# K of the second group multiplied ahead of Q from the weight blocks still in SBUF, with Wo and W1 loaded later and the prologue reordered

## The chip, the cores and the metric

One core of a Trainium2 chip. The metric is the device time of one execution in microseconds; the time of a kernel is the median of its runs. TensorE (PE), VectorE (DVE), ScalarE (ACT) and GpSimd (POOL) each take their own instructions in order; SyncE's queue (SP) issues nearly all DMAs, in order too.

## The reference

x is 128 graphs of 128 nodes with 512 features (f32), adj a 128x128 mask for each graph. Two layers, each with its residual and layer norm:

```
q, k, v = x@Wq + bq, x@Wk + bk, x@Wv + bv              # 8 heads of 64
logits  = where(adj > 0, q@k.T / 8, -1e9)
x = layernorm(x + relu(softmax(logits) @ v @ Wo + bo))

Wh = x @ W1
e  = where(adj > 0, leaky(Wh@a1 [:, None] + Wh@a2 [None, :]), -9e15)
x = layernorm(x + leaky(softmax(e, axis=1) @ Wh))
```

## The kernel before

**Work and stages.** Graphs go in groups of four (512 rows). For group 0 the prologue multiplies Q, K and V in the plain way; for each later group they are made by a two-level Strassen-Winograd scheme. A weight matrix then becomes 49 blocks of 128x128: 7 outer places (`low`/`high`, lines 268 to 315) by 7 inner ones, the sums built once in place. Blocks of Wq stay in SBUF for the whole kernel. Blocks of Wk and Wv are built (`wk.build.0` to `.7` on DVE, `wv.build` on POOL), written to DRAM (`wk.store`, `wv.store`), and fetched back for every group, since the bytes they were built in are used again.

**Where the blocks lie.** Wk is loaded into and built in the tile `late` (`wo_w` in the profile); Wo and W1 go into the same bytes afterwards. Wo's seven places cover exactly `wk.low`, W1's cover `wk.high`. `w.load` issues the four loads of Wo, `w.w1_load.n` those of W1 (and two of its vectors a), `w.block.n` builds Wo's four further places on DVE. Wv is built in `arena`.

**The chains.** A group is six chains, numbered c: two for each matrix (r = 0 with four inner products for each outer one, r = 1 with three, the remainder). `chain_name` says which matrix. A chain has seven outer products in the order p1, p5, p6, p2, p7, p4, p3 (`STEPS`), into three PSUM banks named y, w and x (tags a, b, c, turned by c). Copies from the y bank (t0, t2, t3, c21) are ScalarE's; sums (c11, c22, c12) are DVE's; p6 follows on p1 in the bank y and needs t0 read, p7 needs t2, p4 needs t3. When a chain is done, 3 to 6 combinations finish its output. r = 0 of the first matrix keeps its second half in a spare tile, because the four graphs of the group before still read the output tile.

**Fetches.** `fetch_until` fetches the blocks of chains that are `streamed`: before, K and V of every group from the second on, one or two places at a time, 256 to 512 KB (r = 0) or 192 to 384 KB (r = 1), three ahead.

**Order of work.** Nothing is scheduled by a program at run time: `BEGIN`, a text of some 500 tokens, is the order in which the prologue's instructions are issued, and each engine takes its own in that order. The tokens that matter here:

- `y.q.n.half`, `y.k.n`, `y.v.b`: group 0's products on TensorE; `y.oq.n`, `y.ok.n`, `y.ov.b`: ScalarE's copies of them. n = 2o + j: product n reads of the places 2o and 2o+1 the inner columns j and j+2 (`turned_product`, line 1354). Banks are those of the chains for n < 3, another one for n = 3.
- `wk.build.0` (line 288): inner column 1 minus column 0 in the outer places 0 to 3, in place; `.1` to `.4` whole places (512 wide); `.5` to `.7` further inner columns (896 wide).
- `bN.load`, `bN.turn`: x of graph N fetched and turned on DVE; `bN.masks`, `bN.cast`, `bN.mask`: the adjacency fetched (two graphs at once), cast on ScalarE, made a mask on DVE.
- `sN.scores` (TensorE, 16 matmuls), `sN.add` and `sN.reduce` (DVE: mask and maximum), `sN.exp`, `sN.divide` (ScalarE, by heads), `sN.reciprocals` (DVE), `sN.store`/`sN.fetch`/`sN.transpose` (through DRAM), `sN.attend` (TensorE): attention of graph N.
- `g1.n`, `i1.sNa`, `i1.sNb`: sums of the second group's x that its chains read, on POOL, or on DVE with `.v`.
- `h`: the next product of the chains; `a`, `d`: the next of ScalarE's and DVE's pieces left by it; `k`, `k.v`: the next combination on POOL or DVE; `q`: the next fetch.
- `zN.p1` and so on: Wo's product for a pair of graphs (layer 0's end); `zN.by`, `zN.bw` set its biases in a bank.

After the prologue a steady loop with its own order runs to the end; its text is not touched.

The lines that say which blocks a product reads:

```
block = w.place(2 * o + c // 2).rearrange("p (c f) -> p c f", c=2)
... block[:, c % 2, j * P : (j + 1) * P]                       # group 0

return ring[c, f"p{n + 1}"][:, (0, 1, 2, 0, 3, 1, 2)[m], :]    # a chain, from fetched blocks
```

Of the kernel before, what the change touches and what calls it, by code (L numbers as in the profile page):

```python
# [20 lines left out]
BIG = -1e30  # L21

BEGIN = """
    y.q.1.0 y.q.0.0 y.order.2 b0.masks y.order.3 y.rows.2 y.rows.3 y.q.2.0 y.q.1.1 y.q.2.1
    y.k.3 y.k.1 b4.load.1 y.oq.1 b1.cast b0.cast y.oq.2 b5.load.2 y.k.2 b6.load.0 b2.masks
    w.bias y.q.3.0 y.q.0.1 y.q.3.1 b4.turn wk.build.0 b5.turn b6.turn b7.load.1 wk.build.1
    wk.build.2 wk.build.3 b3.cast wk.build.4 b0.mask b2.cast y.k.0 b1.mask b7.turn
    wk.build.5 y.ok.3 y.oq.0 y.ok.1 y.oq.3 y.ok.2 y.ok.0 wq.scale.3 wq.scale.2 g1.0
    b8.load.2 b4.masks wq.scale.0 wq.scale.1 g1.2 g1.1 b9.load.0 s0.scores wk.build.6
    wk.build.7 s0.add.1 s0.add.0 g1.3 i1.s1a i1.s1b s1.scores s0.reduce s1.add.1 s1.add.0  # L30
    s1.reduce b2.mask wq.build.0 s0.exp.6.7 s0.exp.0.1 s0.exp.2.3 s0.exp.4.5 wk.store.0
    wk.store.2 i1.s3a s0.reciprocals.1 wq.build.1 s0.reciprocals.0 i1.s3b.v wq.build.2 y.v.1
    y.v.3 y.v.0 y.v.2 wk.store.1 wk.store.3 wq.build.4 wq.build.3 w.load w.w1_load.2
    w.w1_load.0 q q b10.load.1 i1.s2a.v i1.s2b w.w1_load.7 q b6.masks w.w1_load.4 wq.build.5
    wq.build.6 b3.mask i1.s4a.v i1.s4b h s2.scores s0.divide.0.1 s1.exp.5.6 s1.exp.2 b4.cast
    s1.exp.7 s1.exp.3.4 s0.divide.4.5 s0.divide.6.7 b5.cast s1.exp.0.1 s0.divide.2.3
    s1.reciprocals.1 b5.mask w.block.0 wq.build.7 w.w1_load.5 s0.store w.w1_load.1
    w.w1_load.6 s1.divide.6.7 b8.turn s1.reciprocals.0 w.w1_load.3 h b11.load.2 y.ov.1
    y.ov.0 y.ov.2 b6.cast a s0.fetch b7.cast s1.divide.4.5 wv.build.0 wv.build.1 h
    wv.build.2 s1.divide.0.1 s1.divide.2.3 a b6.mask s2.add.1 b10.turn s2.add.0 s2.reduce h  # L40
    h h s2.exp.0.1 s2.exp.4.5 a a s2.exp.2.3 d w.halve d s0.transpose b4.mask b11.turn
    s2.reciprocals.0 b9.turn h s3.scores h h h h s0.attend wv.build.3 wv.build.4 wv.build.5
    q s1.store wv.store.2 wv.store.0 s2.exp.6.7 a wv.build.6 wv.build.7 s2.divide.2.3 z0.bw
    s2.divide.0.1 a z0.by wv.store.1 wv.store.3 h h a a s1.fetch h d s3.add.0 s3.add.1 d
    s2.reciprocals.1 k.v w.block.1 k.v d h h s3.reduce a h d b7.mask w.block.2 k.v w.block.3
    q k k k s0.copy s2.divide.6.7 s2.divide.4.5 a h h s1.transpose s3.exp.2 s3.exp.0.1
    y.ov.3 a s3.exp.5.6 z1.by s3.exp.3.4 w.w1_load.8 w.w1_load.9 d d w.w1_sum.3 w.w1_sum.2
    z0.p2 h h s1.attend h a s3.exp.7 a q s2.store g2.0 q q q s3.reciprocals.0 s2.fetch k k.v
    k k.v w.w1_sum.5 s3.reciprocals.1 b1.residual s3.divide.2 s1.copy s1.sum.0 s1.sum.1
    s1.sum.2 z0.p1 h h h s3.divide.3.4 z1.bw z0.t0 s3.divide.7 s3.divide.0.1 a s3.divide.5.6  # L50
    d z0.p5 h w.w1_sum.0 d w.w1_sum.6 k.v w.w1_sum.1 a z0.p6 d z0.c11 z0.t2 k s1.sum.3
    s2.transpose g2.1 k h z0.p7 h h d a z0.t3 a z0.p4 s2.attend z0.c22 k.v z0.c21 s2.copy k
    z0.p3 s3.store b0.residual q z0.stats.1 z0.rstd.1 s3.fetch z0.c12 z1.p1 z0.stats.0 k
    g2.2 q q q k g2.3 z0.apply.1 s3.transpose h h s4.scores s4.add.0 s4.add.1 s3.attend
    z0.rstd.0 z1.t0 a h h s3.copy s4.reduce s4.exp.4.5 s4.exp.0.1 w.w1_sum.4 s5.scores
    b12.load.2 q z0.store.1 b3.residual q h a s4.exp.2.3 s3.sum.0 s4.exp.6.7 s3.sum.1
    s3.sum.2 d z0.apply.0 d w.w1_sum.8 s5.add.1 s5.add.0 s4.reciprocals.1 h a a h s3.sum.3
    z1.p6 h z1.p5 h w.w1_sum.9 s4.reciprocals.0 s5.reduce i2.s1b d w.w1_sum.7 s4.divide.4.5
    s4.divide.6.7 k.v i2.s1a.v k.v s4.divide.0.1 s4.divide.2.3 z1.t2 z1.p7 s5.exp.3.4
    s5.exp.6.7 z1.t3 z0.store.0 q h i2.s3b s5.exp.2 a s4.store s5.exp.5 s5.exp.0.1 z1.p4 h  # L60
    i2.s2a z0.fetch_both a s4.fetch d w.w1_sum.11 i2.s3a.v s5.reciprocals.1 h z1.c21
    w.w1_block.0 s5.reciprocals.0 z1.c22 d h k.v s5.divide.2 s5.divide.7 s5.divide.3.4
    s5.divide.0.1 h s5.divide.5.6 i2.s2b z1.p3 z1.p2 a a i2.s4a s5.store h z1.stats.1 q
    b2.residual d z0.transpose.0 b12.turn h h s4.transpose z1.c11 w.w1_sum.10 k.v k.v k k
    s5.fetch a h z0.transpose.1 z1.rstd.1 w.w1_block.1 s4.attend d z0.sum.0 z0.sum.2 a
    b13.load.0 z1.c12 d i2.s4b w.w1_block.3 z0.sum.1 q q b14.load.2 h h h h s4.copy a a
    z1.stats.0 s5.transpose s5.attend s5.copy d z1.rstd.0 z1.apply.1 k.v k.v z0.sum.3
    s5.sum.0 b13.turn s5.sum.2 w.w1_block.2 z1.store.1 s5.sum.1 k s5.sum.3
"""

STEADY = {
# [94 lines left out]
def kernel(  # L166
# [84 lines left out]
    PLACE = (0, 1, 3, 6, 2, 5, 4)  # L251
# [67 lines left out]
    wq = Weights(const.tile([P, 49 * P], F32, name="wq"))  # L319
    OUTER = 7 * D  # L320
    late = const.tile([P, 2 * OUTER + 14], F32, name="wo_w1")
    wk = Weights(late)
# [3 lines left out]
    wv = Weights(arena)  # L326
# [80 lines left out]
    X, XT, XS, INNER, Q, K, V, MF, OT, X1T, X1, WH = ({} for _ in range(12))  # L407
# [175 lines left out]
        return [step(names) for names in ORDER]  # L583

    def chain_name(c):
        return "QKV"[c % 6 // 2]

    OUT = {"Q": Q, "K": K, "V": V}
    outputs = {
# [12 lines left out]
    def sequence():  # L602
# [10 lines left out]
    streamed = [  # L613
        (c, name)
        for c, name in all_steps
        if c >= 6 and c % 6 >= 2 and name in ("p1", "p5", "p2", "p4")
    ]
    place_in_stream = {step: j for j, step in enumerate(streamed)}

    def fetch_until(last):  # L620
        while fetched[0] <= min(last, len(streamed) - 1):
            c, name = streamed[fetched[0]]
            r = c % 2
            names = (name,) if name == "p1" else (name, CHAIN[CHAIN.index(name) + 1])
            at = [PLACE[PRODUCTS[n]] for n in names]
            low, high = min(at), max(at)
            blocks = work.tile([P, 2, 4, P], F32, name="w_n", bufs=AHEAD + 1)
            for n, place in zip(names, at):
                ring[c, n] = blocks[:, int(place > low)]
            src = stored["w" + chain_name(c).lower(), r][low : high + 1 : max(high - low, 1)]  # L630
            nc.sync.dma_start(blocks[:, : len(at), : 4 - r, :], src.rearrange("n p i f -> p n i f"))
            fetched[0] += 1

    def cells(c):

        g, name = c // 6, chain_name(c)
        if c % 2 == 0:
            if g not in OUT[name]:
                OUT[name][g] = outputs[name]

            def place(h, o):
                if h == 0 or name != "Q":
                    return OUT[name][g][:, h, :, o, :]
                if c not in spare_cells:
                    t = work.tile([P, 2, 3, 2, P], F32, name="cells")
                    flat = t.rearrange("p h s o t -> p (h s o t)")[:, : 8 * P]
                    spare_cells[c] = flat.rearrange("p (s o t) -> p s o t", s=4, o=2)
                return spare_cells[c][:, :, o, :]

            return place  # L650
        if c not in spare_cells:
            spare_cells[c] = work.tile([P, 2, 3, 2, P], F32, name="cells")
        return lambda h, o: spare_cells[c][:, h, :, o, :]

    def group_product(c):
        g, r, name = c // 6, c % 2, chain_name(c)
        count = 4 - r
        outer_tile = {}
# [5 lines left out]
        def weight(n, m):  # L664
            if name == "Q":
                return wq.inner(m)[:, PLACE[n], :]
            return ring[c, f"p{n + 1}"][:, (0, 1, 2, 0, 3, 1, 2)[m], :]

        def multiply(p, n, start):
            j = place_in_stream.get((c, f"p{n + 1}"))  # L670
            if j is not None and not steady[0]:
                fetch_until(j + AHEAD)
            operand = INNER[g][1]
            for index, m in enumerate(ROUNDS[r]):
                xs = operand(n, INNER_PLACE.index(m))
                w = weight(n, m)
                lhs, rhs = (xs, w) if name == "V" else (w, xs)
                nc.tensor.matmul(  # L678
                    p[:, index, :],
                    lhs,  # L680
                    rhs,
                    start=start and index == 0,
                    stop=True,
                    skip_group_check=True,
                )
# [1066 lines left out]
```

## Time and profile before

| | |
|---|---|
| median of three runs | 2266.84 us (2261.54 to 2272.79) |
| the profiled execution | 2263.41 us, span 2261.6 us |
| granted TensorE clock, mean | 0.998 |
| DMA | 540.78 MB, mean 239 GB/s |
| first 300 us: PE busy | 288.39 us |
| first 300 us: DMA | 73.40 MB, 245 GB/s |
| Wo's loads issued | 40.41 to 44.15 us |
| first fetch of K's blocks | 46.50 us |
| first product of the second group | 54.67 us |

A line of the waits view says who waited for whom: us in total, times, the longest. A line of the timeline has the start, the length, engine, line, operation, output<-inputs, shape, count, and in brackets the idle time before it with what ended it. Matmuls of f32 take two instructions for one logical product of 128 rows.

### The profile page before, as it was taken

What the parts mean: (1) busy time and instruction counts of PE and PEld (TensorE: products, weight loads), DVE (VectorE), ACT (ScalarE), POOL (GpSimd) and SP (SyncE); (2) the same over time, 40 slices, a digit from 0 to 9 for tenths busy, and PEclk for the clock granted to TensorE, in tenths of its full rate; (3) what the DMA queues carried; (4) which work ended last, traced back from release to release, by engine and by line L of the source; (5) the groups of instructions that cost most, each with busy time, mean ns of one, the idle gap of its engine ahead of it and who ended that gap; (6) DMA issues with size and microseconds to landing.
All of it is one profiled execution on the core that took longest, in us unless ns stands there. A gap on an engine that the chain in (4) does not pass through costs nothing.

```text
span 2261.6 us, 52550 instructions
## 1 busy us (share of the span) xinstructions
PE 2236.6 (99%) x17228; PEld 2015.0 (89%) x17228; DVE 2014.3 (89%) x4225; ACT 1661.6 (73%) x5955; POOL 1406.2 (62%) x1697
## 2 busy tenths in 40 slices
PE   9899999999999999999999999999999999999998
PEld 6889999999999999999899999999999999999985
DVE  5889999999988999988999889999899988899977
ACT  3668777677677787776776777877767767778786
POOL 2666666656766566666567665666665676556656
PEclk9999999999999999999999999999999999999999
DMA  9988788887888888888888888888888888888764
GB/s 230 273 238 239 237 245 248 240 249 231 243 244 250 247 239 239 241 247 242 235 237 245 241 249 246 239 239 246 244 241 247 235 243 239 250 247 237 219 214 151
DMA packets 516592, 540.78 MB, mean 239 GB/s; under 512 B 100568, under 2 KB 394336, under 8 KB 516320
## 3 DMA queue, kind: packets, MB, share of 16 engines
q1 hardware_dynamic: 516000, 537.17, 81.3%
q8 instruction: 137, 2.24, 0.4%
q14 instruction: 135, 1.11, 0.2%
q10 hardware_dynamic: 320, 0.26, 0.0%
HBM read 388.96 MB, written 148.31 MB: 238 GB/s over the span
## 4 chain that ended last, share of the span: by engine, by line
PE 89%; DMA 4%; DVE 4%; ACT 1%; SPq 1%; issue 1%; POOL 0%; POOLq 0%; DVEq 0%; ACTq 0%
PE st_y L678 24%; PE p_y L798 19%; PE st_w L678 12%; PE p_w L798 9%; PE st_x L678 6%; PE lg L872 6%; PE p_oT L952 5%; PE p_x L798 5%; PE p_h L1207 4%; DMA adj<-in_adj_dram 1%; DMA paz<-pa_dram 1%; DMA w_n<-wv 0%; SPq L933 0%; ACT pa L920 0%; DVE pa L939 0%
## 5 line engine op out<-in xcount | busy, mean ns | idle before, releaser
L906 ACT ACTIVATE pa<-pa,nmax 128x128 f32<-128x128 f32 x1000 | 391.8, 397 | 11.7 <-DVE nmax L895 9.4
L920 ACT ACTIVATE pa<-pa,rs 128x128 f32<-128x128 f32 x1000 | 327.2, 401 | 4.1 <-DVE rs L916 4.1
L728 POOL TENSOR_TENSOR out_Q<-out_Q,cells 128x512 f32<-128x512 f32 x92 | 116.2, 1277 | 297.4 <-DVE out_Q L728 297.4
L691 ACT COPY cells<-st_y 128x384 f32<-128x384 f32 x279 | 133.0, 477 | 102.6 <-PE st_y L678 101.9
L967 ACT ACTIVATE arena<-p_oT,b_cols 128x128 f32<-128x128 f32 x504 | 138.1, 382 | 80.6 <-PE p_oT L952 79.7
L906 ACT ACTIVATION_READ_ACCUMULATOR pa<-pa,nmax 128x1 f32 x1000 | 193.4, 193 | 0.0
L1008 POOL TENSOR_TENSOR rstd<-ve,mhalf 128x1 f32<-128x1 f32 x256 | 161.4, 631 | 21.3
L1000 DVE BATCH_NORM_STATS2 st<-arena 128x6 f32<-128x512 f32 x248 | 168.8, 681 | 1.2
L1006 POOL TENSOR_SCALAR ve<-mv 128x1 f32<-128x1 f32 x256 | 76.1, 297 | 147.7 <-DVE mv L1002 145.0
L886 DVE TENSOR_TENSOR pa<-lg,mf 128x512 f32<-128x512 f32 x250 | 161.5, 675 | 3.7 <-PE lg L872 3.7
L939 DVE STREAM_TRANSPOSE pa<-paz 128x1024 f32<-128x1024 f32 x125 | 154.6, 1236 | 7.0 <-DMA w_n<-wv 3.0
L895 DVE TENSOR_REDUCE nmax<-pa 128x8 f32<-128x1024 f32 x125 | 151.0, 1208 | 1.2
L872 PE MATMUL lg<-out_K,out_Q 64*128 64x128 f32 x2048 | 139.6, 281 | 0.7 <-ACT out_K L1391 0.7
L872 PEld LDWEIGHTS lg<-out_K,out_Q 64*128 64x128 f32 x2048 | 125.2, 187 | 14.3 <-issue 7.2
L728 POOL TENSOR_TENSOR out_K<-out_K 128x512 f32<-128x512 f32 x62 | 79.1, 1275 | 91.1 <-DVE out_K L728 91.1
L712 DVE TENSOR_TENSOR cells<-st_w,cells 128x384 f32<-128x384 f32 (+1 forms) x217 | 120.9, 557 | 16.6 <-ACT cells L691 16.3
L798 PE MATMUL p_y<-wo_w,x1T 128*128 128x257 f32 x496 | 134.2, 393 | 0.0
L1214 ACT ACTIVATE arena<-p_h 128x512 f32<-128x512 f32 x120 | 71.9, 599 | 83.8 <-DMA out_dram<-arena 60.2
L798 PE MATMUL p_y<-wo_w,arena 128*128 128x256 f32 x504 | 131.3, 383 | 0.9 <-ACT pr_t L809 0.9
L1021 DVE TENSOR_SCALAR arena<-arena,mv,rstd 128x512 f32<-128x512 f32 x239 | 131.2, 549 | 0.6 <-POOL rstd L1008 0.6
L798 PE MATMUL p_y<-wo_w,oS 128*128 128x256 f32 x504 | 129.8, 380 | 0.1
L798 PE MATMUL p_y<-wo_w,x1S 128*128 128x257 f32 x496 | 128.2, 380 | 0.2 <-ACT arena L809 0.2
(301 smaller groups left out, 7720.8 us busy)
## 6 DMA issues: line engine op xcount, KB each, us to landing
paz<-pa_dram SPq DMA_DIRECT2D x504, 128.0 KB, 3.6
pa_dram<-pa SPq DMA_DIRECT2D x125, 512.0 KB, 3.8
w_n<-wk SPq DMA_DIRECT2D x93, 512.0 KB, 4.3
w_n<-wv SPq DMA_DIRECT2D x93, 512.0 KB, 5.1
w_n<-wk SPq DMA_DIRECT2D x93, 384.0 KB, 4.3
w_n<-wv SPq DMA_DIRECT2D x93, 384.0 KB, 3.5
x_dram<-arena SPq DMA_DIRECT2D x128, 256.0 KB, 2.6
xz<-x_dram SPq DMA_DIRECT2D x240, 128.0 KB, 3.8
```

Source lines behind the costliest of these rows:

```text
L678: nc.tensor.matmul(p[:, index, :], lhs, rhs, start=start and index == 0, stop=True, skip_group_check=True,)
L728: (by or engine).tensor_add(*(t(n) for t, n in (dst, left, right)))
L798: nc.tensor.matmul(p[:, :width], xs()[n][:, kc, :], w[:, PLACE[n], kc, :], start=start and kc == 0, stop=True, skip_group_check=True,)
L872: nc.tensor.matmul(self.lg[r][:, c, :], q[rows, 2 * (b % 2) + c % 2, c // 2, :], k[rows, 2 * (b % 2) + c % 2, c // 2, :], start=c == 0, st ...
L886: nc.vector.tensor_add(by_head[:, r * NC : (r + 1) * NC], self.lg[r].rearrange("p c (b k) -> p c b k", b=4), mf.unsqueeze(1).to_broadcast( ...
L895: nc.vector.tensor_reduce(self.nmax, by_head, AX.XY, ALU.max, negate=True)
L906: nc.scalar.activation(self.pa[:, :, h, :], self.pa[:, :, h, :], AF.Exp, bias=self.nmax[:, h : h + 1], accum_out=self.sums[:, h : h + 1],)
L920: nc.scalar.activation(self.pa[:, :, h, :], self.pa[:, :, h, :], AF.Copy, scale=self.rs[:, h : h + 1])
L939: nc.vector.transpose(self.paT.rearrange("p h (a i) -> p a h i", i=32), self.paz.rearrange("p a (h k) -> p a h k", k=32),)
L967: nc.scalar.activation(OT[pair][:, c, h * P : (h + 1) * P], self.oT[:, c, :], AF.Identity, bias=b_cols[:, 1, c : c + 1],)
L1000: nc.vector.bn_stats(st, self.src)
L1008: nc.gpsimd.tensor_tensor(self.r, ve, mhalf, ALU.pow)
```

## The change

1. `chain_name`: the second group (c = 6 to 11) takes its matrices in the order K, Q, V, all other groups Q, K, V as before.
2. K's two chains of the second group (c = 6, 7) read the blocks of `wk` where they were built; `streamed` begins with c = 8 and leaves out Q, so eight fetches go.
3. The spare tile for the second half goes with the first chain of a group, whichever matrix it is.
4. `BEGIN` has a new order. Wo and W1 are loaded after K's chains of the second group, which read the bytes they go to. Eight `q` are gone, three `k.v` are `k`, and `i1.s1b`, `i1.s2b`, `i1.s4b` carry `.v`; all other tokens are the same ones in another order.

```diff
 BEGIN = """
-    y.q.1.0 y.q.0.0 y.order.2 b0.masks y.order.3 y.rows.2 y.rows.3 y.q.2.0 y.q.1.1 y.q.2.1
-    y.k.3 y.k.1 b4.load.1 y.oq.1 b1.cast b0.cast y.oq.2 b5.load.2 y.k.2 b6.load.0 b2.masks
-    w.bias y.q.3.0 y.q.0.1 y.q.3.1 b4.turn wk.build.0 b5.turn b6.turn b7.load.1 wk.build.1
-    wk.build.2 wk.build.3 b3.cast wk.build.4 b0.mask b2.cast y.k.0 b1.mask b7.turn
-    wk.build.5 y.ok.3 y.oq.0 y.ok.1 y.oq.3 y.ok.2 y.ok.0 wq.scale.3 wq.scale.2 g1.0
-    b8.load.2 b4.masks wq.scale.0 wq.scale.1 g1.2 g1.1 b9.load.0 s0.scores wk.build.6
-    wk.build.7 s0.add.1 s0.add.0 g1.3 i1.s1a i1.s1b s1.scores s0.reduce s1.add.1 s1.add.0
...
+    y.q.0.0 y.q.1.0 b0.masks y.order.2 y.rows.2 y.order.3 y.rows.3 y.q.2.0 y.q.2.1 y.q.0.1
+    y.q.1.1 y.k.3 y.q.3.0 y.k.1 b6.load.0 w.bias b5.load.2 b4.load.1 b2.masks y.k.2 y.q.3.1
+    y.oq.2 wq.scale.1 b0.cast y.oq.0 y.oq.1 b1.cast wq.scale.0 b2.cast b3.cast y.ok.2 y.oq.3
+    wq.scale.2 y.ok.3 y.ok.1 b6.turn b4.turn b9.load.0 b7.load.1 y.k.0 wk.build.0 b5.turn
+    wk.build.1 wk.build.2 wq.scale.3 y.ok.0 wk.build.3 wk.build.4 wk.build.5 wk.build.7
+    b3.mask b7.turn b0.mask s0.scores s1.scores s0.add.0 s0.add.1 y.v.1 y.v.0 wk.store.1
+    b8.load.2 s0.reduce b1.mask s1.add.0 s1.add.1 wq.build.0 wk.store.0 b4.masks b10.load.1
+    s0.exp.4.5 s0.exp.6.7 s0.exp.2.3 s0.exp.0.1 s0.reciprocals.1 s1.reduce s0.reciprocals.0
+    wq.build.1 g1.2 g1.0 g1.1 g1.3 i1.s1a s0.divide.4.5 s0.divide.6.7 s0.divide.2.3
+    s1.exp.5.6 s1.exp.2 y.v.2 y.v.3 s0.divide.0.1 i1.s2a.v i1.s1b.v wq.build.2 b4.cast
+    s1.exp.7 s1.exp.3.4 y.ov.0 i1.s3a wk.build.6 wq.build.3 b5.cast s1.exp.0.1 wq.build.4
+    i1.s4a.v wq.build.5 i1.s2b.v s2.scores h h wq.build.7 i1.s4b.v b2.mask s1.reciprocals.1
+    b8.turn s1.reciprocals.0 w.halve s2.add.0 s2.add.1 s0.store y.ov.1 s1.divide.4.5
+    s1.divide.6.7 s1.divide.2.3 s1.divide.0.1 y.ov.2 a h wk.store.3 s0.fetch b6.masks
+    wv.build.0 s2.reduce wv.build.1 wv.build.2 a z0.by s2.exp.2.3 s2.exp.6.7 s2.exp.4.5
+    wk.store.2 b11.load.2 h h s2.exp.0.1 b6.cast a s1.store s0.transpose i1.s3b.v
+    s2.reciprocals.1 d s2.reciprocals.0 b10.turn b9.turn b4.mask d wv.build.4 wv.build.3
+    s0.attend h h s3.scores h a s2.divide.2.3 y.ov.3 h h z1.bw a b7.cast s2.divide.0.1 a
+    s2.divide.6.7 z0.bw h h h wv.build.5 a s2.divide.4.5 a wv.build.7 wv.build.6 wv.store.2
+    wv.store.0 h wv.store.1 s1.fetch d k.v k.v d s3.add.1 s3.add.0 k.v d h b11.turn
+    s3.reduce d h h a wv.store.3 s1.transpose b5.mask wq.build.6 s0.copy s3.exp.0.1 a h h
+    s1.attend s3.exp.5.6 s3.exp.2 s3.exp.3.4 w.load k k k g2.0 a s3.exp.7 s1.copy k s1.sum.0
+    s2.store w.w1_load.2 w.w1_load.1 w.w1_load.3 w.w1_load.5 w.w1_load.8 w.w1_load.0
+    w.w1_load.9 d k.v w.block.0 k.v k.v s1.sum.2 s1.sum.1 z0.p1 h h z0.p2 s3.reciprocals.1
...
     def chain_name(c):
-        return "QKV"[c % 6 // 2]
+        return ("KQV" if c // 6 == 1 else "QKV")[c % 6 // 2]
...
-        if c >= 6 and c % 6 >= 2 and name in ("p1", "p5", "p2", "p4")
+        if c >= 8 and chain_name(c) != "Q" and name in ("p1", "p5", "p2", "p4")
...
-                if h == 0 or name != "Q":
+                if h == 0 or c % 6:
                     return OUT[name][g][:, h, :, o, :]
...
             if name == "Q":
                 return wq.inner(m)[:, PLACE[n], :]
+            if c < 8:
+                return wk.inner(m)[:, PLACE[n], :]
             return ring[c, f"p{n + 1}"][:, (0, 1, 2, 0, 3, 1, 2)[m], :]
```

More of the change, by code (lines that the diff above doesn't have):

```diff
@@ L30 @@
-    wk.build.7 s0.add.1 s0.add.0 g1.3 i1.s1a i1.s1b s1.scores s0.reduce s1.add.1 s1.add.0
[L31 to L65, printed above, removed]
@@ L66 @@
-    b13.load.0 z1.c12 d i2.s4b w.w1_block.3 z0.sum.1 q q b14.load.2 h h h h s4.copy a a
-    z1.stats.0 s5.transpose s5.attend s5.copy d z1.rstd.0 z1.apply.1 k.v k.v z0.sum.3
-    s5.sum.0 b13.turn s5.sum.2 w.w1_block.2 z1.store.1 s5.sum.1 k s5.sum.3
+    y.q.0.0 y.q.1.0 b0.masks y.order.2 y.rows.2 y.order.3 y.rows.3 y.q.2.0 y.q.2.1 y.q.0.1
+    y.q.1.1 y.k.3 y.q.3.0 y.k.1 b6.load.0 w.bias b5.load.2 b4.load.1 b2.masks y.k.2 y.q.3.1
+    y.oq.2 wq.scale.1 b0.cast y.oq.0 y.oq.1 b1.cast wq.scale.0 b2.cast b3.cast y.ok.2 y.oq.3
@@ new lines @@
+    s1.attend s3.exp.5.6 s3.exp.2 s3.exp.3.4 w.load k k k g2.0 a s3.exp.7 s1.copy k s1.sum.0
+    s2.store w.w1_load.2 w.w1_load.1 w.w1_load.3 w.w1_load.5 w.w1_load.8 w.w1_load.0
+    w.w1_load.9 d k.v w.block.0 k.v k.v s1.sum.2 s1.sum.1 z0.p1 h h z0.p2 s3.reciprocals.1
+    w.block.1 s3.reciprocals.0 d w.block.2 h s3.divide.2 z0.t0 a a s3.divide.7 s3.divide.5.6
+    s3.divide.3.4 s3.divide.0.1 h z0.p6 h a s2.fetch w.w1_load.4 w.w1_load.7 q w.w1_load.6
+    s3.store b1.residual h h z0.p5 w.block.3 z0.c11 d b6.mask k.v w.w1_sum.1 d z0.t2 a d
@@ new lines @@
+    s2.transpose w.w1_sum.6 w.w1_sum.2 w.w1_sum.3 s1.sum.3 z0.p7 h h z0.t3 z1.by a a z0.p4 h
+    s2.attend d z0.c22 w.w1_sum.0 k k g2.1 z0.c21 q b0.residual h k.v k z0.stats.1 z0.p3 h
+    z0.c12 s4.scores s3.fetch q w.w1_sum.5 s2.copy a z0.rstd.1 s4.add.0 s4.add.1
+    s3.transpose z1.p1 h h k g2.2 k s3.attend z0.apply.1 z0.stats.0 s5.scores s3.copy z1.t0
+    a s4.reduce q b12.load.2 q q z0.store.1 s4.exp.0.1 s4.exp.6.7 s4.exp.2.3 h z1.p2 h
+    z0.rstd.0 g2.3 s3.sum.0 s3.sum.2 s3.sum.1 d s5.add.1 z0.apply.0 s4.exp.4.5 a a d b7.mask
@@ new lines @@
+    z1.c11 h q b3.residual z0.store.0 z1.p6 s4.reciprocals.0 w.w1_sum.4 s4.reciprocals.1 d
+    s5.add.0 s5.reduce s4.divide.6.7 s4.divide.4.5 z1.t2 s4.divide.0.1 w.w1_sum.7 k s3.sum.3
+    s4.divide.2.3 z1.p5 h h q z0.fetch_both i2.s1a.v w.w1_sum.11 k.v i2.s2a k i2.s1b i2.s2b
+    z1.p7 h s5.exp.5 a z1.t3 s5.exp.3.4 s5.exp.6.7 h z1.c22 z1.p4 i2.s4a s5.exp.2 a
+    s5.exp.0.1 s5.reciprocals.1 d z1.c21 w.w1_sum.9 s5.reciprocals.0 d w.w1_sum.10
+    z1.stats.1 z0.transpose.1 h h h s5.divide.5.6 s5.divide.0.1 s5.divide.7 s5.divide.3.4
@@ L69 @@
+    s5.divide.2 s4.store b2.residual z1.p3 a s4.fetch h h d z0.transpose.0 w.w1_sum.8
+    s5.store a a z1.rstd.1 k.v k.v s4.transpose i2.s3a.v b12.turn h h s4.attend h b13.load.0
+    s5.fetch z1.apply.1 d k k a a z1.c12 d z1.stats.0 h h w.w1_block.0 i2.s4b i2.s3b
+    s5.transpose d z0.sum.2 z1.rstd.0 z0.sum.0 a s4.copy h z0.sum.1 w.w1_block.1 s5.attend
+    s5.copy k w.w1_block.2 w.w1_block.3 s5.sum.0 s5.sum.1 z0.sum.3 s5.sum.2 q q q b14.load.2
+    z1.store.1 s5.sum.3 k k b13.turn
 """
```

## The prediction

> **What bounds the kernel now.** I read the page first, then TensorE's waits in the first 300 us, then the windows round the longest of them, and last the timeline of 24 to 66 us, where the change acts.
>
> ```profile
> span 2261.6 us, 52550 instructions
> ...
> PE 2236.6 (99%) x17228; PEld 2015.0 (89%) x17228; DVE 2014.3 (89%) x4225; ACT 1661.6 (73%) x5955; POOL 1406.2 (62%) x1697
> ...
> PE   9899999999999999999999999999999999999998
> ```
>
> TensorE is the bound: it idles 25.0 us of 2261.6. Everything the change touches lies in the first two or three of the forty slices (56.5 us each). Its waits there:
>
> ```profile
> PE st_y L678 <- ACT out_Q L697: 2.1, 1, 2.1
> PE st_w L678 <- DVE cells L712: 1.5, 1, 1.5
> PE p_busy L1316 <- POOL ident masks.py:199: 1.3, 1, 1.3
> PE st_y L678 <- DVE cells L712: 1.3, 1, 1.3
> PE st_y L678 <- ACT out_V L1412: 1.0, 1, 1.0
> PE p_oT L952 <- DVE arena L939: 0.9, 1, 0.9
> PE st_y L678 <- DVE out_K L712: 0.9, 1, 0.9
> PE lg L872 <- ACT out_K L1391: 0.7, 1, 0.7
> ```
>
> With four shorter ones and a few cracks the timeline's gaps add up to 11.6 us by 145.8 us: 1.3 at the start, 3.9 more up to 60.15, 6.3 after. No DMA is a releaser: the fetches that the change removes stop TensorE only through other engines. One does: at 59.0 ScalarE has waited 3.9 us for a mask (adj) that lay behind the loads of Wk's blocks, Wo and W1, and the 2.1 us wait is behind that. It is followed by a half clock:
>
> ```profile
> 58.20:61.60 3.40, 1.45 (x12) 1.45 (x13) 2.26 (x4) 2.59 (x10) 3.24 (x4) 0.97 0.74 208
> 61.60:65.00 3.40, 3.33 (x16) 3.04 (x16) 3.33 (x4) 2.88 (x14) 3.32 (x2) 0.52 0.76 196
> ```
>
> (columns: length, busy time of PE, PEld, DVE, ACT, POOL, granted clock, DMA share, GB/s). 3.4 us at 0.5 cost 1.7. So all that can be won is 10.3 of gaps and 1.7 of clock, 12.0 us or 0.53%.
>
> **Part 1, the four K products and DVE's first build.** This is the step that I count on.
>
> ```profile
> 24.67 3.70 PE L1360 MATMUL st_x<-xT,wo_w 128*128 128x512 f32 x8
> 26.92 1.02 PE L1360 MATMUL st_x<-xT,wo_w 128*128 128x512 f32 x2
> 27.55 0.69 DVE L288 TENSOR_TENSOR wo_w<-wo_w 128x512 f32<-128x512 f32 x1 [2.34 <-PE st_x L1360]
> 32.83 5.20 DVE L288 TENSOR_TENSOR wo_w<-wo_w 128x896 f32<-128x896 f32 x3
> 33.38 3.60 PE L1360 MATMUL st_y<-xT,wo_w 128*128 128x512 f32 x8
> 38.87 1.29 DVE L886 TENSOR_TENSOR pa<-lg,mf 128x512 f32<-128x512 f32 x2 [0.83 <-PE lg L872]
> 41.44 0.40 ACT L906 ACTIVATE pa<-pa,nmax 128x128 f32<-128x128 f32 x1 [1.75 <-DVE nmax L895]
> 60.15 0.49 PE L678 MATMUL st_y<-xS,wq 128*128 128x128 f32 x2 [2.13 <-ACT out_Q L697]
> ```
>
> wk.build.0 (27.55) changes in place only column 1 of places 0 to 3. k.2 reads columns 0 and 2 of places 2 and 3, none of them; yet DVE idled 2.34 us for it. It started when the sixth of k.2's eight matmuls ended (26.92 + 0.59 = 27.51): the third block, place 3 column 0, the last that lies between the first and the last address the build writes. So the wait goes by the range of addresses, not by the cells. Before, k.0 is issued after this build. In the new order y.k.0 stands ahead of it, and three of k.0's four blocks (place 0 column 2, place 1 columns 0 and 2) lie in that range. DVE must then wait for k.0, the last of the stage, which ended at 36.98.
>
> k.0 itself: the eight Q halves and four K products are the same work in another order, but ScalarE now casts mask 0 ahead of y.oq.1, whose bank k.1 needs. The mask came at 23.53; cast 0.3, then oq.0 and oq.1 at 0.6 each: k.1 starts at about 25.1 where TensorE is there at 24.4. +0.7, k.0 ends at 37.7.
>
> Behind the waiting build on DVE: four builds, two x turns (7 instructions at 0.65 with the build itself, 4.5), two 896-wide builds (1.0 each: the row of wq has 1.08 without GpSimd beside it; the 5.20 for three above is with it), two small mask steps (0.2): 6.7. The first score add comes at 44.4, not 38.87; with 1.25 and 1.15 for adds and maximum the first exp at 46.9, not 41.44.
>
> GpSimd waits too: its sums of the new group's x need the last turn (44.3). Before, five sums took 32.99 to 41.82, 8.8: now to 53.1. Only then can DVE go on: i1.s2a.v, four more inner sums and six builds, eight of them 512 or 384 wide (five at 0.65, three at 0.5) and three 896 wide (1.0), 7.8 in all, and a mask: s1.reciprocals at 61.0. ScalarE, idle by then, does eight divides (2.45, as a row at 110.17 has it), y.ov.2 (0.55) and the first copy t0 of the K chain (0.6): 64.6. The third product, p6, needs that copy.
>
> TensorE meanwhile: V to 54.35 (before 53.65), s2.scores 1.09, p1 and p5 1.35 each: ready for p6 at 58.1, waits until 64.6, 6.5 us in pieces. In before the same work (with s2.scores) stood at 60.15. **+4.5.**
>
> Had the hold cost nothing, DVE could build from k.2's end on and GpSimd sum from 38, all of it 6 us earlier: p6 at 58.6, a gain of 1.5, and no half clock. These are the two ends; I take +4.5, because the wait at 27.55 is a row of the very instruction that is moved.
>
> **Part 2, clock.** In before 2.1 us of idle was followed by half clock, 1.7. The new idle is longer; I take the same 1.7, so 0 between the two; bounds −1.7 and +1.7 (a second such stretch).
>
> The Trainium skill (TensorE: Matmul & The Clock Gate, Part 1) says that the clock falls after at least one idle window of about 3.4 us, by windows that run freely. Before's gap of 2.1 us should then have cost nothing and only the new one would: by the rule this part would be +1.7, by the row 0. Here the row decides.
>
> **Part 3, K ahead of Q without fetches.** The chain's matmuls take 0.39 for two and 0.61 for four whether from wq or w_n, so from wk too: 0. The three-piece copy with bias moves with Q: 0. Eight fetches go (256 + 3×512 and 192 + 3×384 KB, 3.2 MB; at the 274 to 290 GB/s of the windows from 40 to 60 us 11 to 12 us of DMA, and eight issues of about 0.4 on SP). TensorE waited for none, so 0; the mask behind them is counted in part 1's rival end. DVE takes three inner sums (0.5, 0.5, 0.5) and gives three combinations (0.4 to 0.7) to GpSimd: 0, bounds ±1.
>
> **Part 4, Wo and W1 behind.** Issued only when K's last product has read wk. By the same walk K1's last product ends near 81, and first needed is Wo's place 0, by z0.p1, after four Q products and s1.attend, 6.4 later. Place 0 may load as soon as K's first remainder product has read it, near 73. Cover enough: 0. The loads landed in 6.6 us (median); SP's queue has wv.store ahead, which waits for GpSimd's last wv.build (67.5 before, some 69 now). If SP came only after 81, z0.p1 would wait up to 6.6: bounds 0 and +6.6. The eight W1 loads and the dots behind them are needed only by the steady loop, with 40 us of room.
>
> **Part 5, the rest of the prologue.** Gaps of 6.3 after 60.15 in before. New ones that the walk shows: K1's remainder p1 behind DVE's c11, which stands behind s2.reciprocals (0.5 to 1.5); Q's p5 behind ScalarE's c21 (0.7); wq.build.6 between Q's p6 and p2 (0.1, by the same address ranges); z0.bw needs a bank that s3.add frees, as in before (1.3 there). I can't follow it to the end, and take the old 6.3 over: 0, bounds −6.3 and +6.
>
> **Sum**: 2263.41 (profiled execution) + 4.5 = 2267.9. The median shown is 3.4 above that execution, so **2271.3**.
>
> **Rivals.**
> - *The hold is not there* or hidden: −1.5, −1.7, and half of the later gaps, −3.1: 6.3 off, 2260.5. For it: ScalarE idles 1.75, 2.5 and 3.9 us in before, cover that could take up some lateness; the late mask goes. Against: the 2.34 us row.
> - *Slower by over 0.5%*: the late softmaxes are not caught up. DVE's c11 and c22 of the K chain stand behind s2.reciprocals, so behind eight exps (3.1) and two turns and a mask (1.4), and TensorE's next products behind them; with a bank for z0.bw (2.0, ScalarE's wait at 73.2 in before) and a second half clock (1.7): 4.5 + 8.2 = 12.7, 2279.5. Decides if s2's exps begin after about 69; the walk has 66. Against: ScalarE is only 39 to 61% busy in three of the five slices from 50 to 100 us.
> - *It does little*: late and early steps cancel, −3 to +2.
>
> **How the numbers follow.** Forecast (+2 to +10): 0.48. Hold absent (−3 to −12): 0.25, of it 0.04 beyond 11.3. Little: 0.10. Not caught up (over +10): 0.17, of it 0.14 beyond 11.3. Half a percent, 11.3 us, is about what a measurement of this kernel can tell from no change (its three runs lie 11 apart). Faster 0.04, within 0.82, slower 0.14. Range 2257 (the first rival's gain and its noise) to 2281 (the second at its price).
>
> **What would show it.** Right: wk.build.0 on DVE idle until k.0 ends (37 to 38), the first exp near 47, TensorE idle for some 5 us before the K chain's p6 near 60 to 65, then half clock. Wrong: the first exp by 42, no gap over 1 us between 54 and 66; then it is faster. If TensorE waits for a DMA of Wo, part 4 failed; if the idle after 66 is far from 6.3, part 5.

## The result and the profile after

The changed kernel takes 2279.51 us (median of six runs, 2277.30 to 2284.34) against 2267.51 us for six runs of the kernel before beside it: ratio 1.0059, interval 1.0043 to 1.0074, so 0.6% slower. Its profiled execution took 2277.30 us, span 2275.5 us. The page of after, answering to the first lines shown of before:

```profile
span 2275.5 us, 52536 instructions
...
PE 2236.7 (98%) x17228; PEld 2015.3 (89%) x17228; DVE 2020.6 (89%) x4225; ACT 1659.2 (73%) x5955; POOL 1408.7 (62%) x1697
...
PE   9699999999999999999999999999999999999998
```

TensorE does the same work (2236.7 us busy, 2236.6 before); the span is 13.9 us longer, and the second slice has fallen from 8 tenths to 6. All the loss is idle time of TensorE there. Its waits in the first 300 us, the view of the prediction's second fence (us in total, times, the longest):

```profile
PE st_w L680 <- DVE inner_s L497: 8.4, 1, 8.4
PE st_y L680 <- ACT out_K L693: 7.6, 1, 7.6
...
PE st_y L680 <- DVE out_K L714: 0.6, 1, 0.6
```

Two waits that before does not have. Up to 320 us TensorE is idle for 25.7 us in after and 11.6 in before (320 less its busy time in the windows view, 294.33 and 308.39), and the difference, 14.1, is that of the spans to 0.2. Split at the third product of the second group (p6, which before stood at 60.15): 0.6 us more ahead of 58, 8.37 + 7.61 at p6's door where before had 2.13, and 5.9 behind it where before had 6.3. The timeline of after, all engines, the lines that carry this:

```profile
37.82 0.69 DVE L288 TENSOR_TENSOR wo_w<-wo_w 128x512 f32<-128x512 f32 x1 [8.61 <-PE st_y L1362]
...
47.49 0.40 ACT L908 ACTIVATE pa<-pa,nmax 128x128 f32<-128x128 f32 x1 [9.09 <-DVE nmax L897]
...
58.46 1.59 POOL L257 TENSOR_TENSOR arena<-arena 128x512 f32<-128x512 f32 x1
58.85 1.74 DVE L259 TENSOR_TENSOR wq<-wq 128x512 f32<-128x512 f32 x1
60.13 1.59 POOL L259 TENSOR_TENSOR arena<-arena 128x512 f32<-128x512 f32 x1
60.52 1.74 DVE L497 TENSOR_TENSOR inner_s<-xT,inner_s 128x512 f32<-128x512 f32 x1
61.68 1.70 POOL L258 TENSOR_TENSOR arena<-arena 128x512 f32<-128x512 f32 x1
62.19 2.15 DVE L288 TENSOR_TENSOR wq<-wq 128x896 f32<-128x896 f32 x1
63.46 8.02 POOL L288 TENSOR_TENSOR arena<-arena 128x896 f32<-128x896 f32 x3
64.26 2.42 DVE L497 TENSOR_TENSOR inner_s<-inner_s,xS 128x384 f32<-128x384 f32 x1
66.60 2.96 DVE L288 TENSOR_TENSOR wq<-wq 128x896 f32<-128x896 f32 x1
66.73 0.80 PE L680 MATMUL st_w<-inner_s,wo_w 128*128 128x128 f32 x2 [8.37 <-DVE inner_s L497]
...
71.92 0.16 DVE L918 RECIPROCAL rs<-sums 128x4 f32<-128x4 f32 x1
75.57 0.79 PE L680 MATMUL st_y<-xS,wo_w 128*128 128x128 f32 x2 [7.61 <-ACT out_K L693]
```

Read it from the top. wk.build.0 (37.82) had DVE idle for 8.61 us, until k.0 ended at 37.79: this wait, "the hold" from here on, is there, and the first exp comes at 47.49. Then look at lengths: DVE's 512-wide sums last 1.74 us instead of 0.68, the 896-wide builds 2.15 to 2.96 instead of 1.08, a 384-wide sum 2.42 instead of 0.54, and each start stands 0.4 to 0.8 us behind the start of an instruction of GpSimd (its builds of Wv). The engine counts as busy all the while. So the inner sum that TensorE needs for p5 (64.26) ends at 66.7, s1.reciprocals come at 71.92, ScalarE (idle 14.5 us for them) divides until 74.5, copies, and p6 starts at 75.57. The same stretch by windows (length; busy time of PE, PEld, DVE, ACT, POOL; granted clock; DMA share; GB/s):

```profile
50.00:60.00 10.00, 7.41 (x39) 4.16 (x37) 10.00 (x11) 7.58 (x32) 8.72 (x6) 1.00 0.58 184
60.00:70.00 10.00, 1.22 (x4) 0.93 (x4) 10.00 (x6) 0.00 (x0) 9.69 (x6) 0.60 0.60 145
70.00:80.00 10.00, 4.43 (x24) 4.42 (x24) 7.06 (x11) 5.71 (x20) 1.48 (x1) 0.55 0.53 176
```

From 60 to 70 us DVE is busy for all ten, for six instructions; ScalarE does nothing, TensorE 1.2 us. The clock is at half from 62.0 to 79.1, but most of that falls on idle time.

### The profile page after: what moved, and what is told of

Same layout as the page of the kernel before. It is cut to its first block, busy times and chain, and to the rows that moved or that the text cites. A ratio compares the mean times of both kernels' runs of the same rounds, so it can differ in the third digit from the quotient of the medians.

```text
span 2275.5 us, 52536 instructions
## 1 busy us (share of the span) xinstructions
PE 2236.7 (98%) x17228; PEld 2015.3 (89%) x17228; DVE 2020.6 (89%) x4225; ACT 1659.2 (73%) x5955; POOL 1408.7 (62%) x1697
## 4 chain that ended last, share of the span: by engine, by line
PE 90%; DMA 4%; DVE 3%; ACT 1%; issue 1%; SPq 0%; POOL 0%; DVEq 0%; POOLq 0%; ACTq 0%
PE st_y L680 24%; PE p_y L800 19%; PE st_w L680 12%; PE p_w L800 9%; PE st_x L680 6%; PE lg L874 6%; PE p_oT L954 5%; PE p_x L800 5%; PE p_h L1209 4%; DMA paz<-pa_dram 1%; DMA w_n<-wv 1%; DVE pa L941 1%; DVE inner_s L497 0%; ACT pa L922 0%; ACT pa L908 0%
## 5 line engine op out<-in xcount | busy, mean ns | idle before, releaser
L693 ACT COPY cells<-st_y 128x384 f32<-128x384 f32 (+1 forms) x281 | 133.9, 476 | 103.6 <-PE st_y L680 101.9
L954 PE MATMUL p_oT<-pa,out_V 128*64 128x128 f32 x2000 | 125.3, 276 | 2.9 <-DVE pa L941 2.7
```

The source lines that it names most:

```text
L954: nc.tensor.matmul(self.oT[r * HD : (r + 1) * HD, c, :], v[:, c % 2, c // 2, r * HD : (r + 1) * HD], self.paT[:, r * NC + c, :], start=c == 0,
```

## The experiments

Theory A: two things together make the loss, the hold (a wait by the range of addresses) and, once the hold has pushed DVE's sums and builds back beside GpSimd's builds of Wv, the two engines slowing each other. Rival B: the hold alone, with work that is simply late. Rival C: not the hold, but K ahead of Q with the late loads. Each run gives a ratio to runs of before on the same chip beside it; "gaps" are TensorE's idle time up to 320 us in its profiled execution (before 11.6, after 25.7), p6 is the third product of the second group. Gaps are of one execution and ratios of medians whose runs lie 10 us and more apart, so ratios within 0.2% of each other need not follow the gaps (e1 and e7).

| kernel | ratio | interval | gaps, us | p6 starts |
|---|---|---|---|---|
| after | 1.0059 | 1.0043 to 1.0074 | 25.7 | 75.57 |
| e1 | 1.0015 | 1.0001 to 1.0029 | 15.0 | 56.95 |
| e2 | 0.9996 | 0.9985 to 1.0008 | 14.1 | 59.16 |
| e3 | 1.0016 | 1.0001 to 1.0031 | 17.0 | 65.41 |
| e4 | 1.0031 | 1.0019 to 1.0043 | 21.2 | 64.43 |
| e5 | 1.0043 | 1.0027 to 1.0058 | 17.5 | 57.86 |
| e6 | 1.0024 | 1.0006 to 1.0041 | 18.6 | 56.53 |
| e7 | 0.9997 | 0.9980 to 1.0013 | 17.0 | 59.18 |
| e8 | 1.0005 | 0.9990 to 1.0020 | 11.9 | 56.77 |
| e9 | 1.0006 | 0.9991 to 1.0022 | 13.5 | 61.16 |
| e10 | 1.0031 | 1.0012 to 1.0050 | 16.0 | 57.88 |
| e11 | 1.0043 | 1.0025 to 1.0061 | 18.0 | 57.88 |

**e1_split_build0**: the build in four subtractions of one place each, the order of after kept.

```diff
         def first(self, engine, *outer):
-            return self.difference(engine, 1, 1, 0, *outer)
+            cuts = [(n, n + 1) for n in range(*outer)] if self is wk else [outer]
+            return lambda: [self.difference(engine, 1, 1, 0, *cut)() for cut in cuts]
```

> wk.build.0 is cut into four subtractions, one for each outer place, each over one unbroken stretch of addresses; the order of everything stays that of the changed kernel. Theory (the wait goes by the range of addresses): the first of them no longer waits for k.0 and starts by 30 us instead of 37.8, the first exp comes at 41.5 to 43 instead of 47.5, p6 of the K chain by 60, no stretch at half clock, time 2257 to 2264 (0.995 to 0.999 of before). Rival A (the whole tile is waited for): build at 37.8, time as the changed kernel's, 2279. Rival B (the hold matters little; GpSimd and VectorE side by side are the cause, and would be without it): exp early, but p6 still after 66, time 2272 or more.

The timeline of e1:

```profile
29.61 0.85 DVE L288 TENSOR_TENSOR wo_w<-wo_w 128x128 f32<-128x128 f32 x4
...
51.72 1.08 DVE L288 TENSOR_TENSOR wq<-wq 128x896 f32<-128x896 f32 x1
...
56.95 0.49 PE L680 MATMUL st_y<-xS,wo_w 128*128 128x128 f32 x2 [0.30 <-ACT out_K L693]
...
76.39 1.14 ACT L969 ACTIVATE arena<-p_oT,b_cols 128x128 f32<-128x128 f32 x4 [3.09 <-DMA wv<-arena]
```

The same cells change, in the same place of the order, and DVE no longer waits for any product: the range, not the cells, made the wait. DVE's later pieces have their usual lengths (1.08), since GpSimd's Wv builds start at 53.66, when DVE is through with them, and p6 stands at 56.95. The loss falls to about a quarter (0.15%, interval 0.01 to 0.29). The time that was expected, a gain, did not come, and a half clock did (78.86 to 82.27): TensorE now waits 1.33 us at 60.96, 1.27 at 68.83 and 2.82 at 76.30. The last is ScalarE's copy of s0 (76.39), which waits for the store of Wv and keeps Q's copy behind it.

**e2_build0_before_k0**: the same hold taken away by order.

```diff
-    ... b7.load.1 y.k.0 wk.build.0 b5.turn ...
+    ... b7.load.1 wk.build.0 y.k.0 b5.turn ...
```

> One token moved: wk.build.0 stands ahead of y.k.0, as in the kernel before; all else as in the changed kernel. Theory: wk.build.0 waits for k.2's third block only and starts near 31 to 32; the same result as cutting it up, within 2 us, 2257 to 2265. Rival A predicts the same here, since k.0 is out of the way, so A and the theory part only at the cut kernel. Rival B: 2272 or more.

```profile
31.13 0.69 DVE L288 TENSOR_TENSOR wo_w<-wo_w 128x512 f32<-128x512 f32 x1 [2.29 <-PE st_x L1362]
```

The timeline shows the wait of before again (2.29 us, for k.2). The ratio is 0.9996: one token moved gives the whole loss back, and K is still ahead of Q with the loads late, so C is not the cause of it. The gain beyond it, which was expected, is not there: 2.31 us of waiting remains at p6, and 8.8 us behind it.

**e3_wq_builds_late**: the hold stays, four builds of DVE leave the stretch.

```diff
-    ... wq.build.3 ... wq.build.4 ... wq.build.5 ... wq.build.7 ... i1.s3b.v
+    ... i1.s3b.v wq.build.3 wq.build.4 wq.build.5 wq.build.7
```

> The hold stays (build at 37.8, first exp at 47.5). Four builds of Wq (3, 4, 5, 7), which the Q chains need only after 88 us, are moved on VectorE's queue behind s0.transpose and i1.s3b. Theory (what stands ahead of s1.reciprocals on VectorE's queue sets p6): the 8.6 us that they took there go, s1.reciprocals at 62 to 64 instead of 71.9, p6 at 66 to 68 instead of 75.6, time 2269 to 2273. Rival C (ScalarE or the fetches set p6): p6 moves by less than 3 us, time 2277 or more.

s1.reciprocals at 61.76 and p6 at 65.41, though the pieces that are left are still slow (1.75, 2.15, 1.61 and 1.50 us). Ten microseconds come back at p6, as expected; the whole is 1.0016.

**e4_gpsimd_held**: the hold stays, DVE's list stays, GpSimd may not start on Wv before s1.reciprocals. The added instruction writes a spare tile.

```diff
         def build(self, n):
+            self.w is wv and n == 0 and nc.gpsimd.tensor_scalar_add(ready, jobs["s1"].rs[:, 0:1], EPS)
             self.builds[n]()
```

> The hold stays. One tiny GpSimd instruction that reads the result of s1.reciprocals is put ahead of wv.build.0, so that GpSimd builds nothing while VectorE works through its chain. Theory (the eleven long VectorE instructions from 55 to 72 us are stretched by GpSimd's builds beside them): they fall back to 0.5 to 0.7 (512 and 384 wide) and 1.1 (896 wide), s1.reciprocals near 61 to 62 and p6 near 65, which is what the prediction had; time 2268 to 2272, if the later end of the Wv builds (75 instead of 71.5) costs nothing. Rival D (they are slow for another reason, the half clock or DMA traffic): they stay at 1.7 and 2.2 or more, p6 after 73, time 2278 or more.

The timeline of e4:

```profile
57.14 0.68 DVE L497 TENSOR_TENSOR inner_s<-xT,inner_s 128x512 f32<-128x512 f32 x1
57.74 1.08 DVE L288 TENSOR_TENSOR wq<-wq 128x896 f32<-128x896 f32 x1
58.74 0.54 DVE L497 TENSOR_TENSOR inner_s<-inner_s,xS 128x384 f32<-128x384 f32 x1
...
60.78 0.16 DVE L918 RECIPROCAL rs<-sums 128x4 f32<-128x4 f32 x1
...
64.43 0.80 PE L680 MATMUL st_y<-xS,wo_w 128*128 128x128 f32 x2 [4.37 <-ACT out_K L693]
...
85.26 1.14 ACT L969 ACTIVATE arena<-p_oT,b_cols 128x128 f32<-128x128 f32 x4 [3.79 <-DMA wv<-arena]
```

This is the experiment that tells A from B. The three instructions of after at 60.52, 62.19 and 64.26 took 1.74, 2.15 and 2.42 us; with GpSimd idle they take 0.68, 1.08 and 0.54, and s1.reciprocals come 11.1 us earlier. B is out: lateness alone would not have changed lengths. Only half of the time comes back. The hold's own price stays (1.16 us at p5 and 4.37 at p6, where before had 2.13), and Wv is now stored late, so that s0's copy waits 3.79 us for it (85.26): a gap of 3.5 us at Q's p6 and another half clock. The time that was expected counted on no such wait.

**e5_k_first_old_order**: K ahead of Q, no fetches, Wo and W1 behind, but BEGIN as it was before.

In words: BEGIN is that of before without its first eight `q`; `w.load` stands behind K's last product, `w.w1_load.*` ahead of `z1.by`, `w.block.*` behind `s1.attend`.

> The code of the changed kernel with the order of before: only the loads of Wo and W1 and Wo's blocks are moved behind K's last product of the second group, and eight fetch tokens dropped. It is the change without its reordering of the prologue. Theory (the reordering, by the hold and what it pushes together, is the whole loss; K first by itself is free or gains): first exp at 41 to 42, no hold; the mask that ScalarE waited 3.9 us for comes sooner, so the gap of 2.1 us and the half clock at 60 go; 0.997 to 1.000 of before, that is 0 to 7 us faster. Rival E (K first itself costs: Wo lands late for z0, or K's early copies crowd ScalarE): 1.002 or more.

The timeline of e5:

```profile
87.03 0.42 DVE L379 SCALAR_TENSOR_TENSOR wa_scr<-wo_w,arena 128x256 f32<-128x256 f32 x1 [7.20 <-DMA pa_dram<-pa]
...
94.93 0.79 PE L680 MATMUL st_x<-xT,wq 128*128 128x128 f32 x2 [7.33 <-DVE out_Q L714]
```

The wait of 2.1 us at p6 is gone, and there is no hold. But DVE's first dot of W1 (`w.w1_sum.3`, a product with a vector a) stands at its old place and needs W1 and that vector, now issued on SP at 75.5 to 83.2 (the releaser the view names is another transfer of that moment); 7.20 us of DVE, and Q's c12 (94.22) is queued behind. Without the reordering, too, the change is 0.4% slower.

**e6_mended**: four repairs at once: e2's, e3's, s0.copy behind s1.attend, and y.oq.0 and y.oq.1 ahead of b0.cast.

```diff
-    ... b0.cast y.oq.0 y.oq.1 ... y.k.0 wk.build.0 ... s0.copy s3.exp.0.1 ...
+    ... y.oq.0 y.oq.1 b0.cast ... wk.build.0 y.k.0 ... s1.attend s0.copy ...
```

> The changed kernel with four repairs of order: wk.build.0 ahead of y.k.0; Wq's builds 3, 4, 5, 7 behind s0.transpose; s0.copy, which waits until the Wv blocks are stored, behind s1.attend, so that the copies of the Q chain do not stand behind it; y.oq.0 and y.oq.1 ahead of the first cast. Theory: p6 of the K chain by 57.5, no gap over 1.5 us before 90 us, no half clock; TensorE's gaps to 320 us fall from 14.0 (build moved alone) to 9 to 11; 0.997 to 0.999 of before. Rival F (each repair brings up the next wait at the same price): gaps stay at 13 or more, 0.9995 to 1.001.

The timeline of e6:

```profile
63.50 5.72 DVE L288 TENSOR_TENSOR wq<-wq 128x896 f32<-128x896 f32 x2
...
70.03 0.77 PE L680 MATMUL st_y<-xT,wo_w 128*128 128x128 f32 x2 [9.48 <-DVE rs L918]
```

The builds that were moved out of one stretch stand now beside the Wv builds (53 to 68 us here), take 10.0 us instead of some 3.5, from 59.2 to 69.2, and K's next product waits 9.48 us for the c11 behind them. p6 came by the time expected (56.53), but at 1.0024 both the theory and rival F are missed. My mending rebuilt the fault one stage later: the contention without the hold.

**e7_split_copy_late**, **e8_split_copy_c11**, **e9_before_split**: e1 with s0.copy behind s1.attend; that with K's first c11 ahead of s2.reciprocals; and the kernel before with e1's split alone.

```diff
-    ... s0.copy s3.exp.0.1 ... s1.attend                 # e7, e8
+    ... s3.exp.0.1 ... s1.attend s0.copy
-    ... s2.reciprocals.1 d s2.reciprocals.0              # e8
+    ... d s2.reciprocals.1 s2.reciprocals.0
```

> The split of e1 (wk.build.0 in four one-place subtractions) with s0.copy moved behind s1.attend. In e1 TensorE's longest gap was 2.82 us at 76.30, where Q's p6 waited for ScalarE's copy of out_Q, queued behind s0.copy, which itself waited 3.09 us for the store of Wv; a half clock (3.4 us) began just before it. Theory (that wait is the price of an earlier prologue that meets a store whose time has not moved): the gap and the half clock go, 2.8 + 1.7 = 4.5 us, so the ratio falls from 1.0015 to about 0.9995, gaps to 320 us to 12. Rival (the time is only handed on: s1.attend or Q's next product then waits for the bank or the mask instead): gaps stay at 14 or more and the ratio at 1.001 or above.

> As e7_split_copy_late, and DVE's c11 of the K chain's first remainder goes ahead of both s2.reciprocals, where it stood between them. Theory (the prediction's item in part 5: K's p1 behind c11 behind s2.reciprocals, 1.33 us at 60.96 in e1): that gap goes, ratio 0.0006 below e7's, about 0.999. Rival (the two x turns and the mask behind it hold the next adds anyway): the gap is only moved to the next product, ratio as e7's.

> The kernel before with nothing but the split of wk.build.0 into four one-place subtractions. There the build waited 2.34 us for k.2. Theory (in the old order that wait lies beside DVE's and ScalarE's own idle time and the late mask sets p6): the build starts some 2 us earlier, and the time stays within 0.1%: ratio 0.999 to 1.001, p6 within 0.5 us of 60.15. Rival (the address-range wait already cost the old order time): ratio 0.998 or less, p6 before 59.

(By the windows e1's half clock lay at 78.86 to 82.27, from the end of that gap on, not before it as e7's text has it; e5's, in e10's text, lay at 79.01 to 82.42 and 92.66 to 99.49.) In e7 the copy no longer waits and there is no half clock, but in this execution TensorE waits 1.90 us at p6 and 1.55 at 84.16, so that the gaps, 17.0, are those of its rival and the ratio, 0.9997, that of the theory. In e8 those two gaps are not there, and the 1.33 us behind c11 have become 1.01 us behind a copy of ScalarE (61.65); no half clock, 11.9 us in all, but 1.0005 where 0.999 was expected. Neither ratio shows a difference from before. e9: in the old order the build starts at 25.86, 1.7 us earlier, and nothing follows from it (p6 at 61.16, for it waits for the mask; 0.8 of the 1.0 us by which this misses the expected 60.15 stand already at the first scores, 38.49 for 37.66): in the old order the wait at the build cost nothing that shows.

**e10_k_first_sums_late**, **e11_k_first_sums_spread**: e5 with DVE's dots of W1 moved, first three behind a fourth, then five spread out.

```diff
-    ... w.w1_sum.3 w.w1_sum.2 z0.p2 ... w.w1_sum.5 ... w.w1_sum.1
+    ... z0.p2 ... w.w1_sum.1 w.w1_sum.3 w.w1_sum.2 w.w1_sum.5            # e10
+    ... z0.c22 w.w1_sum.1 ... z0.c21 w.w1_sum.6 ... z0.stats.1 w.w1_sum.3 ... # e11
```

> e5_k_first_old_order with its first three dots of W1 (w.w1_sum.3, .2, .5) moved behind w.w1_sum.1, so that DVE no longer waits for W1 and the vector a ahead of Q's pieces. In e5 that was 7.20 us of DVE at 79.83 to 87.03 and 7.33 us of TensorE at 87.60, with 6.8 us of half clock at 85.3. Theory (K ahead of Q without fetches costs nothing by itself in the order of before; what it costs is where the loads moved behind it are met): the long gap and its half clock go, 7.3 + 3.4 us, and the ratio falls from 1.0043 to 0.999 to 1.001. Rival (Wo itself lands late whatever stands behind it: TensorE already waited 1.1 us for it at 77.87): a wait of 2 us or more takes its place between 78 and 100, ratio 1.002 or more.

> e5_k_first_old_order with five dots of W1 spread out behind the Q chain's pieces on DVE (w.w1_sum.1 behind z0.c22, .6 behind z0.c21, .3, .2 and .5 behind z0.stats.1, z0.stats.0 and s4.add.1). In e10 three of them stood in a row with two others ahead of Q's c22, ten instructions with the last four slowed to 1.36 us beside GpSimd, and TensorE waited 4.97 us at 92.84 for that c22, with a half clock of 3.4 us. Theory (K ahead of Q without fetches costs nothing by itself; only where DVE meets the loads moved behind it does): that gap and half clock go, 5.0 + 1.7 us, and the ratio falls from 1.0031 to about 1.000 (0.999 to 1.0015), gaps to 320 us to 11 or less. Rival (another instruction of DVE waits for a late load or another gap of 2 us or more takes its place before 110): ratio 1.002 or more.

The 7.33 us at 87.60 are gone in both, and another wait takes their place: 4.97 us at 92.84 in e10 (a piece of the Q chain on DVE behind eight dots in a row, three of them slowed from 0.42 to 1.36 us beside GpSimd, not ten and four as e11's text has it), 5.59 us at 102.00 in e11 (an attend that waits for DVE's transpose, with eight dots among the pieces ahead of it). Both expectations failed on the side of their rivals: in the old order the work that the late loads push back falls on DVE among the pieces that TensorE needs between 80 and 108 us (in e10 DVE also still waits 2.02 us for the vector a, at 87.72). Whether some order gives it room stays open; no order that was run beats the kernel before.

## Why the prediction was right in part and wrong in its size

The time, 2279.51, lies inside the range (2257 to 2281) and 8.2 us above the forecast; the 0.6% is just beyond the half percent to which I gave 0.14. The sign and the place were right, one term was mis-sized. That the range holds the result is in part luck: its upper end was the price of a rival whose mechanism was not the one.

- **What bounds the kernel, and what could be won**: right. Even e8, with no half clock and its named gaps gone, has 11.9 us of gaps where before has 11.6.
- **Part 1, the hold**: right, to 0.6 us: k.0 ends at 37.79 (37.7), first score add 44.91 (44.4), first exp 47.49 (46.9). e1 and e2 show that it goes by addresses and is where the loss begins.
- **Part 1, the chain behind it: the step that failed.** The prediction priced "four more inner sums and six builds" at 0.65, 0.5 and 1.0 us, 7.8 in all, for s1.reciprocals at 61.0 and p6 at 64.6. Measured, where GpSimd ran beside them (nine of the eleven): 1.7, 2.4 and 2.2 to 3.0; s1.reciprocals at 71.92, p6 at 75.57. With GpSimd held back (e4) they stand at 60.78 and 64.43: the walk was right for an engine alone, and the 11 us between are the price of GpSimd beside it. So p6, forecast 4.5 us later than in before, came 15.4 later, and TensorE's gaps grew by 14.1 (25.7 less 11.6). The row was in view: my fence shows three 896-wide builds of before at 5.20 us, and the working even set it aside as "with it", in favour of 1.08. I moved the list 6 us later and did not ask what GpSimd would be doing by then.
- **Part 2, clock**: within its bounds. 17 us at half, but only some 2.7 us of full-speed work inside, by the lengths at 66.73 and 75.57 to 79.12 (2.1 us lost, 1.7 before). The new idle was longer and the cost nearly the same, as taken. The reading by the row, not the rule of a whole idle window, was the one to take (last section).
- **Part 3, K without fetches**: right, 0: no wait for a fetch, the chain's matmuls at 0.39 and 0.61 at full clock.
- **Part 4, Wo and W1 behind**: right in this order, 0: the loads were issued from 83.94 on, z0.p1 at 96.85 without a gap. Not a property of the change: in e5, e10 and e11 the same loads made waits of 5 to 7 us.
- **Part 5, the rest**: right, 5.9 us behind p6 for 6.3. The item "K1's remainder p1 behind c11" measured 0.62 us.
- **The rival "slower by over 0.5%"**: its price, 12.7, is near the 13.9 of the spans, and its point of decision (s2's exps after 69) was passed, at 78.5. Its mechanism was not the one: 16 us of the waiting stood ahead of p6, on DVE, and only 0.6 on c11 behind the reciprocals.
- **The rival "hold absent"** at −6.3 (ratio 0.997): that kernel is e1 and e2, and they stand at 1.0015 and 0.9996. Half of the later gaps were to go; in e8 the gaps from 100 to 320 us still add up to 4.9, where before has 3.4. Without the hold no gain can be measured: the intervals of e2, e7 and e8 hold 1, and e1's begins just above it.

The Trainium skill has a rule for the step that failed (SBUF — State Buffer, section "SBUF: two separate sides"): VectorE and GpSimd share one pair of ports as a lock, and a DVE instruction with two SBUF inputs and a GpSimd one that reads SBUF take turns, each for its whole length. The trace agrees: between 58.46 and 61.68 both engines' starts lie 1.5 to 1.7 us apart, about GpSimd's 1.27 alone plus 0.4, and the DVE add that has one input in PSUM keeps its 0.65 (47.66, two in 1.29 us, with GpSimd's sums beside).

## What to carry to other kernels

When a step makes an engine's work later, price it beside what the other engines do then, not by its length at its old place: here a list of eleven instructions ran 11 us longer, with the engine "busy" throughout. In this kernel a write over a strided view waited for readers of all that lies between its first and last address (8.61 us for products that read none of its cells); cut into unbroken pieces (e1) or issued ahead of the last of them (e2) it waited 0 and 2.29. What sets the wait, the chip or the program's own semaphores, no run here shows. And before believing a repair, look where the moved work lands: e4, e6, e10 and e11 each took one wait away and made another a stage later.

## What the runs showed of the hardware that was not expected

- DVE beside GpSimd's tensor_tensor (alone 1.27 us for 512, 2.14 for 896 columns): 512 wide 0.68 to 1.74, 896 wide 1.08 to 2.15 or 2.96, 384 wide 0.54 to 2.42, a dot of 256 0.42 to 1.36, and a bf16 mask step of 128 columns 0.19 to 1.29 (54.31 in e7). GpSimd's own go from 1.27 to 1.59 or more. Each of these DVE lengths is the instruction's own plus the whole of the GpSimd instruction beside it, less 0.2 to 0.3 us: 0.68 + 1.27 gave 1.74, 1.08 + 2.14 gave 2.96, 0.54 + 2.14 gave 2.42.
- The half clock went by windows, not by gaps. In every trace here it starts and ends on a grid of 3.41 us, which lies differently in each run. In all thirteen, at full clock, it followed every stretch of that grid in which TensorE idled 1.82 us or more (the least: e4, 86.17 to 89.58) and none in which it idled 1.76 or less (the most: e10, 121.24 to 124.65). So before's gap of 2.13 us brought it, since it lay in one stretch (58.01 to 61.42), and e7's of 1.90, cut by the grid, did not; of two gaps of about 1 us each, 2 us apart, e5's lay in one stretch (75.59 to 79.00) and brought it, e10's in two and did not.
